# A graph network on one core: thresholds compared inside the steps of the norm, one per engine and step, and edges asked for by fours

## The chip, the core and the metric

The kernel runs on one NeuronCore of a Trainium2 chip. Five engines work beside each other, each in the order of its own queue: PE (TensorE, matrix products), DVE (VectorE), ACT (ScalarE), POOL (GpSimd) and SP (SyncE, which here only issues transfers). Transfers run on 16 DMA engines; they are issued by SP, by ACT, and by POOL for indirect ones (gathers by a list of addresses). Semaphores hold an instruction until what it needs is there.

The metric is the device time of one execution in microseconds (us), the median of several runs. Before the change it is 2130.42 us (three runs, 2127.44 to 2132.5).

## The reference, cut to what matters

```python
def agg(h):
    return jax.ops.segment_sum(h[src], dst, num_segments=N)      # N = 6250, 100000 edges, dst sorted

h = jnp.maximum(_layernorm(x), 0.0)                              # x: 6250 x 256
y = h
for l in range(3):
    h = y + agg(y)
    h = relu(h @ W1s[l] + b1s[l]); h = relu(h @ W2s[l] + b2s[l])
    y = h @ W3s[l] + b3s[l]
h = y + agg(y)
h = relu(h @ cW1 + cb1); h = relu(h @ cW2 + cb2)                 # cW2: 256 x 64
return x + h @ cW3 + cb3
```

## The kernel before, in words

The 6250 nodes are 49 blocks of 128. The sum over edges is done as a product with a matrix of edge counts, block by block: `build` makes the counts of a block (128 destinations against all nodes) as products of one-hot rows, `product_by_node` and `product` multiply them with the node values (XY, a high and a low part), and some blocks are gathered instead, by indirect transfers of rows (`Gathered`). The first matrix of each layer is applied ahead of the sum, and W3 of a layer is multiplied with W1 of the next one (`fused`).

All of that needs a preparation, and the change lies in it. Three generators share it; the order in which they are advanced is written out by hand under `tc.manual_schedule()` (from L964 on), and it is the order of each engine's queue.

- `look` finds the edges. It loads the first destination of each 128 edges (`firsts_i`), spreads them over 98 partitions by a product (L652), counts how many lie below each partition's first node (L654) and so finds where a partition's edges begin. Each partition (64 nodes) loads a window of NEAR edges from there with one indirect transfer (`near_i`, L663). In the window it counts, for 17 thresholds four nodes apart, the edges below the threshold: 11 of them on DVE (L695), 6 on ACT by a sign (L698). From the counts come the starts of 16 groups; for each group the destinations and the sources are asked for with `ask` (L611, 32 indirect transfers on POOL), and 14 more for the blocks that are gathered. Lines L720 to L757 place these. Then come four pieces of 4 groups each (L773 to L779, and transposes L786), a check that the list is sorted (L794, L795, on `run`, the whole list), checks of the counts (L800 to L820), and the gathered blocks' addresses (L826 to L845). A violated check sets `wrong`, and a general path then computes everything anew.
- `fused` turns W3 (L575, L577), multiplies it (L586), with the bias as an additional left side (b3b, L579), and copies and stores the result (L588, L589). It runs in six halves.
- `normed` does the layer norm and the first product with W1 over 25 pairs of blocks. In step s it copies the product of pair s-3 out (`out`, L932, every third on ACT, the rest on DVE), splits pair s-4 in a high part (L936, ACT) and a low one (L940, DVE), scales pair s (L899, ACT), transposes pair s-1 (L908, copied by ACT L911), multiplies pair s-2 (L920), takes the moments of pair s+6 (L879, L880, DVE) and stores pair s-5 (SP). `settle` turns moments into scales (L891, L892).

Before, `look` goes through all of its thresholds first, with the halves of `fused` between ACT's six, and then the steps of the norm start; the remaining parts of `look` are put behind single steps (`STAGES`). Each step first asks for two transfers of edges; each waits for the latest product of the norm (`after`), so that they are spread.

Behind the norm's last store, `build` makes the first one and a half blocks (12 batches, 24 copies out of PSUM, L1084 on ACT and L1086 on DVE in turns), and then the products begin.

Loads carry one of eight semaphores, in rotation; an issue waits until the load that had the same one has landed.

Of the kernel before, what the change touches and what calls it, by code (L numbers as in the profile page):

```python
# [8 lines left out]
F32 = mybir.dt.float32  # L9
# [5 lines left out]
OP = mybir.AluOpType  # L15
# [381 lines left out]
def sorted_edges(  # L397
# [63 lines left out]
    NEAR = 11 * P  # L461
# [95 lines left out]
    def fused(pool, w3_aps, w1_aps):  # L557
# [11 lines left out]
        for l in range(NLAYER):  # L569
            w3, w1 = loaded[l]  # L570
            w3t = pool.tile([P, KC, C], F32, name="w3t", bufs=1)
            for k in range(KC):
                ps = ps_m.tile([P, W], F32, name="ps")
                for i in range(KC):
                    nc.tensor.transpose(ps[:, i * P:(i + 1) * P], w3[:, i, k * P:(k + 1) * P],  # L575
                                        ident)
                nc.scalar.copy(w3t[:, k, :], ps[:, :C])  # L577
            b3b = pool.tile([P, KC, P], F32, name="b3b", bufs=1)
            nc.gpsimd.tensor_copy(b3b, b3[l][:, :, None].to_broadcast([P, KC, P]))  # L579
            yield  # L580
            w = pool.tile([P, KC + 1, C], F32, name="w31", bufs=1)
            for i in range(KC + 1):
                ps = ps_m.tile([P, W], F32, name="ps")
                for k in range(KC):
                    left = w3t[:, k, i * P:(i + 1) * P] if i < KC else b3b[:, k, :]
                    nc.tensor.matmul(ps[:, :C], left, w1[:, k, :], start=(k == 0),  # L586
                                     stop=(k == KC - 1))
                nc.scalar.copy(w[:, i, :], ps[:, :C])  # L588
# [28 lines left out]
    def look(pool):  # L617
        firsts_i = pool.tile([1, EB], I32, name="near_i", bufs=1)
        with nc.allow_non_contiguous_dma(reason="each tile's first destination"):
# [6 lines left out]
        nc.sync.dma_start(out=run[:FULL, :], in_=bass.AP(tensor=dst.tensor, offset=dst.offset,  # L626
                                                         ap=[[EC, FULL], [1, EC + 1]]))
        nc.sync.dma_start(out=run[FULL:FULL + 1, :E - FULL * EC],
                          in_=dst[FULL * EC:E].rearrange("(o e) -> o e", o=1))
# [15 lines left out]


        half = pool.tile([P, 2], F32, name="half", bufs=1)
        junk = pool.tile([P, NEAR], BF16, name="junk", bufs=1)
        for h in range(2):
# [3 lines left out]
                             start=True, stop=True)  # L653
            nc.vector.tensor_scalar(junk[:NSUB, e0:e1], ps[:NSUB, :e1 - e0], low[:NSUB, 0:1], None,  # L654
# [11 lines left out]
        )  # L666
        yield
# [24 lines left out]
        DV = 11  # L692
        for q in range(GSUB + 1):
            if q < DV:
                nc.vector.tensor_scalar(junk[:NSUB], near[:NSUB], float(GD * q), None,  # L695
                                        op0=OP.is_lt, op1=OP.add, accum_out=less[:NSUB, q:q + 1])
            else:
                nc.scalar.activation(junk2[:NSUB], near[:NSUB], AF.Sign, bias=edge[:NSUB, q:q + 1],  # L698
                                     accum_out=less[:NSUB, q:q + 1])
                yield  # L700
        nc.vector.tensor_scalar(less[:NSUB, DV:], less[:NSUB, DV:], -0.5, float(NEAR // 2),
                                op0=OP.mult, op1=OP.add)
        first = pool.tile([P, GSUB + 1], F32, name="first", bufs=1)
        nc.vector.tensor_scalar(first[:NSUB], less[:NSUB], at[:NSUB, 0:1], None, op0=OP.add)
        starts = pool.tile([NSUB, GSUB], I32, name="starts", bufs=1)
        nc.vector.tensor_scalar(starts, first[:NSUB, :GSUB], float(E - P), None, op0=OP.min)
        wd = pool.tile([P, GSUB, P], I32, name="wd", bufs=1)
        ws = pool.tile([P, GSUB, P], I32, name="ws", bufs=1)
        for q in range(GSUB):
            for w, e in ((wd, dst), (ws, src)):  # L710
                asks.append((w[:NSUB, q, :], e, starts[:, q:q + 1]))
        ask(4)
# [4 lines left out]
        sel = pool.tile([P, NQ, PW], F32, name="near_i", bufs=1)  # L717
# [113 lines left out]
        yield  # L831
# [27 lines left out]
    def normed(pool, ps_t, ps_z):  # L859
        G = 6  # L860
# [86 lines left out]
        for t0 in range(0, 4 * G, G):  # L947
            load(t0)
        yield
        for s in range(G):  # L950
            moments(s)
        settle(G)
        yield
        for s in range(len(pairs) + 5):
            if s % (G // 2) == 0 and s and s * 2 + 3 * G < NT:
                load(s * 2 + 3 * G)
            for lag, f in ((3, out), (4, high), (0, scale), (1, turn), (2, times), (-G, moments),
                           (4, low), (5, keep)):
                if 0 <= s - lag < len(pairs) and (f is not moments or s - lag >= G):
                    f(s - lag)  # L960
            settle(s + G - 1)
            yield

    with tc.manual_schedule():  # L964
        with tc.tile_pool(name="prep", bufs=2) as prep, tc.tile_pool(
# [88 lines left out]
        def build(hots, ats, ps_b):  # L1054
# [7 lines left out]
            for k, (s, q0) in enumerate(batches):  # L1062
# [6 lines left out]
                for q in range(0, BATCH, 2):  # L1069
# [13 lines left out]
                    if step % 2:  # L1083
# [705 lines left out]
```

## Time and profile before

| | us |
|---|---|
| median of three runs | 2130.42 |
| the profiled execution | 2135.8 |
| its span | 2134.0 |
| first product (L1588) starts | 142.70 |
| first one-hot (L1035) starts | 126.08 |
| first compare with a threshold (L695) | 23.77 |
| first scaling of the norm (L899) | 43.48 |

A row of the timeline gives start, duration, engine, line, operation, output and input with their shapes, and the number of instructions merged into it; in brackets stands the idle time of the engine ahead of it and what ended that. A row of groups gives the count, the busy time, the mean duration of one in ns and the idle time ahead. Consecutive instructions of one engine overlap in the records by about 0.1 us, so that what one costs is better read from its start to the start of the next. A row of windows gives a stretch, the busy time of each engine in it, the granted clock of PE and the use of the DMA engines.

### The profile page before, as it was taken

The numbers are of one execution on the slowest core, as the hardware profiler recorded it, in microseconds if no ns is written. First come the engines' busy times: TensorE is split into PE (matmuls) and PEld (weight loads), VectorE is DVE, ScalarE is ACT, GpSimd is POOL, SyncE is SP. The second block draws the span as 40 slices with busy tenths as digits, with TensorE's granted clock in tenths as the row PEclk, the third lists the DMA queues.
The fourth block names the chain that finished last, engine by engine and source line by source line (L and its number), as shares of the span: only waits on it lengthen the run. The fifth ranks groups of instructions, "written<-read, shape, count | busy, mean of one in ns | idle before, by whom it ended". The sixth has DMA issues, their size and how long they took to land.

```text
span 2134.0 us, 33393 instructions
## 1 busy us (share of the span) xinstructions
PE 2057.4 (96%) x12076; PEld 1487.8 (70%) x12076; DVE 937.7 (44%) x2192; ACT 864.3 (41%) x1775; POOL 1445.4 (68%) x1470
## 2 busy tenths in 40 slices
PE   4979999999999999999999999999999999999997
PEld 3756766667667777777776777777776777777675
DVE  7877867667673422222233322222233433333332
ACT  4856655556556522323232433222333432223231
POOL 2727777777774477777776377777776277777773
PEclk9979999999999999999999999999999999999999
DMA  5524545545455655455455554555456555556553
GB/s 157 176 98 139 162 142 153 158 140 164 150 158 152 213 163 155 153 181 164 142 186 167 173 160 148 173 165 169 146 168 195 170 172 181 184 180 194 183 160 119
DMA packets 184901, 347.61 MB, mean 163 GB/s; under 512 B 32446, under 2 KB 118496, under 8 KB 184726
## 3 DMA queue, kind: packets, MB, share of 16 engines
q0 software_dynamic: 68960, 185.41, 29.7%
q1 hardware_dynamic: 113838, 158.12, 22.3%
q8 instruction: 97, 1.59, 0.3%
q10 hardware_dynamic: 1928, 1.85, 0.3%
q14 instruction: 78, 0.64, 0.1%
HBM read 287.98 MB, written 57.26 MB: 162 GB/s over the span
## 4 chain that ended last, share of the span: by engine, by line
PE 88%; DVE 5%; DMA 4%; issue 1%; ACT 1%; POOL 1%; SPq 0%; DVEq 0%; POOLq 0%; ACTq 0%
PE agg L1665 43%; PE agg L1588 16%; PE sums L1419 11%; PE ps L1233 6%; PE ps L1290 6%; PE bp L1076 4%; DMA rows<-table,idx 3%; PE ps L1479 1%; POOL rows L1382 1%; DVE junk L695 1%; PE bp L920 1%; DVE hi L1035 1%; DVE at L1086 1%; PE ps L1245 0%; DMA table<-zs 0%
## 5 line engine op out<-in xcount | busy, mean ns | idle before, releaser
L1382 POOL DMA_INDIRECT rows<-table,idx x1394 | 1387.7, 995 | 611.4 <-issue 220.6
L1665 PE MATMUL agg<-a,XY 128*128 128x512 f32 x4116 | 982.8, 395 | 1.9 <-DVE clT L1600 1.9
L1665 PEld LDWEIGHTS agg<-a,XY 128*128 128x128 f32 x4116 | 764.6, 188 | 209.5 <-issue 45.8
L1565 ACT CAST a<-at 128x512 fp32r<-128x512 uint8 (+1 forms) x542 | 326.9, 616 | 576.9 <-PE agg L1665 543.9
L1565 DVE CAST a<-at 128x512 fp32r<-128x512 uint8 x543 | 242.7, 448 | 552.8 <-PE agg L1665 469.3
L1588 PE MATMUL agg<-XY,a 128*128 128x512 f32 x1470 | 404.9, 409 | 1.3 <-DVE un L1600 0.7
L1588 PEld LDWEIGHTS agg<-XY,a 128*128 128x128 f32 x1470 | 258.9, 189 | 53.7 <-issue 8.7
L1419 PE MATMUL sums<-rows,hot 128*32 128x256 f32 x3772 | 256.0, 385 | 16.2 <-DMA rows<-table,idx 15.0
L1419 PEld LDWEIGHTS sums<-rows,hot 128*32 128x32 f32 x3772 | 112.6, 109 | 142.6 <-issue 53.6
L1549 ACT CAST a<-at 128x512 fp32r<-128x512 uint8 (+2 forms) x362 | 196.7, 574 | 6.5 <-PE agg L1588 6.5
L1084 ACT CAST at<-bp 128x392 uint8<-128x392 f32 x240 | 116.6, 487 | 203.7 <-PE bp L1076 191.0
L1086 DVE CAST at<-bp 128x392 uint8<-128x392 f32 x240 | 135.1, 563 | 138.2 <-PE bp L1076 138.2
L1448 DVE TENSOR_TENSOR u<-u,sums 128x256 f32<-128x256 f32 x82 | 34.3, 419 | 241.8 <-PE agg L1665 226.9
L1076 PE MATMUL bp<-hi,lo 128*128 128x196 bf16 x960 | 127.5, 255 | 11.0 <-DVE hi L1035 10.7
L1290 PE MATMUL ps<-w,h 128*128 128x256 f32 x588 | 133.9, 379 | 1.4 <-ACT h L1236 0.9
L1233 PE MATMUL ps<-h,w 128*128 128x512 f32 (+3 forms) x332 | 133.9, 545 | 0.6 <-DVE zz L1298 0.6
L1035 DVE TENSOR_TENSOR hi<-cols,pairs 128x784 bf16<-128x784 bf16 x240 | 134.3, 560 | 0.0
L1076 PEld LDWEIGHTS <-lo 128*128 128x128 bf16 x960 | 70.6, 99 | 81.9 <-DVE hi L1035 27.8
L1290 PEld LDWEIGHTS ps<-w,h 128*128 128x128 f32 x588 | 111.1, 190 | 18.7 <-ACT h L1236 1.8
L1483 ACT ACTIVATE h<-ps,bias 128x256 f32<-128x256 f32 (+1 forms) x116 | 47.2, 464 | 154.9 <-PE ps L1479 154.9
L1298 DVE TENSOR_TENSOR zz<-ps,w 128x512 f32<-128x512 f32 (+1 forms) x75 | 50.1, 678 | 117.0 <-PE ps L1290 117.0
L1035 DVE TENSOR_TENSOR lo<-lanes,pairs 128x512 bf16<-128x512 bf16 x240 | 100.3, 418 | 1.3 <-ACT pairs L1030 1.3
(171 smaller groups left out, 989.7 us busy)
## 6 DMA issues: line engine op xcount, KB each, us to landing
at<-mat SPq DMA_DIRECT2D x151, 448.0 KB
mat<-at SPq DMA_DIRECT2D x30, 784.0 KB
rows<-table,idx POOLq DMA_INDIRECT x1394
table<-zz SPq DMA_DIRECT2D x72, 256.0 KB
back<-table SPq DMA_DIRECT2D x99, 128.0 KB
xs<-in_x_dram SPq DMA_DIRECT2D x8, 768.0 KB
table<-zs SPq DMA_DIRECT2D x24, 256.0 KB
out_dram<-zz SPq DMA_DIRECT2D x24, 256.0 KB
```

Of the source, the lines that this page charges most:

```text
L1035: nc.vector.tensor_tensor(o.rearrange("p q (n t) -> p q n t", t=2), values.rearrange("p (n t) -> p n t", t=2)[:, None, :, :].to_broadcast( ...
L1076: mm = nc.tensor.matmul(bp[:, m * HW:(m + 1) * HW], lo[:, q + m, :], hi[:, q + m, :], start=True, stop=True)
L1084: nc.scalar.copy(o, v)
L1086: nc.vector.tensor_copy(o, v)
L1233: mm = nc.tensor.matmul(ps[:mp, :w], weights[l][0][:, c, i * P:i * P + mp], h1[:, c, :w], start=(c == 0), stop=(c == KC - 1))
L1290: mm = nc.tensor.matmul(o, h2[0][:, c, nodes], w3[:, c, :], start=(c == 0), stop=(c == KC - 1))
L1382: got = nc.gpsimd.indirect_dma_start(out=t, out_offset=None, in_=tables[self.l][:, :], in_offset=bass.IndirectOffsetOnAxis(ap=idx[:, o:o + ...
L1419: nc.tensor.matmul(self.sums[m * Q:(m + 1) * Q, :C], self.hot[:, (c - min(rounds)) // 2, m, :], self.rows[g, c + 4 * m], start=(c == ROUND ...
L1549: nc.scalar.copy(a[:, i * m * P:(i + 1) * m * P].rearrange("p (j d) -> p j d", j=m), counts[b][:, j:j + m, :])
L1565: cast(o, at[:, :, d:d + m * P])
L1588: mm = nc.tensor.matmul(agg, a[:, d:d + P], XY[:, j, :], start=(j == 0), stop=(j == NT - 1))
L1665: mm = nc.tensor.matmul(agg[c][:, :w], XY[:, j, o:o + P], a[:, :w], start=(j == 0 and half == 0), stop=(j == NT - 1 and half == 1))
```

## The change

- The window NEAR is 1280 edges for 1408.
- The thresholds are compared inside steps 0 to 7 of the norm, one on DVE (the even ones) and one on ACT (the odd ones) a step, the seventeenth on ACT too. After each second step the four groups that are then known are settled (`settled`, three small instructions) and put on the list to be asked for; a step asks for three in steps 1 to 8 and for two later.
- `fused`'s six halves stand behind steps 0 to 5; the bias is read by the product in place, with stride 0, and the copy b3b goes. The biases are turned in step 1.
- The moments run 4 pairs ahead instead of 6. The first pair's stand ahead of the count of the first destinations, three more behind it; x is loaded in two halves, `run` between them.
- ACT issues W3 and W1 of two layers ahead of the biases, then takes a square root into the first column of `wrong`, which loads its table; `look` clears `wrong` behind that in the program.
- The remaining parts of `look` follow other steps, the gathered blocks two by two. `sel` uses another tile.
- The 24 copies of the first batches in `build` are all on ACT.

```diff
-    NEAR = 11 * P
+    NEAR = 10 * P
...
-            b3b = pool.tile([P, KC, P], F32, name="b3b", bufs=1)
-            nc.gpsimd.tensor_copy(b3b, b3[l][:, :, None].to_broadcast([P, KC, P]))
...
-                    left = w3t[:, k, i * P:(i + 1) * P] if i < KC else b3b[:, k, :]
+                    left = (w3t[:, k, i * P:(i + 1) * P] if i < KC else
+                            b3[l][:, k:k + 1].to_broadcast([P, P]))
...
+        for q in range(0, GSUB, 2):
+            nc.vector.tensor_scalar(junk[:NSUB], near[:NSUB], float(GD * q), None,
+                                    op0=OP.is_lt, op1=OP.add, accum_out=less[:NSUB, q:q + 1])
+            for k in (q + 1,) if q + 2 < GSUB else (q + 1, q + 2):
+                nc.scalar.activation(junk2[:NSUB], near[:NSUB], AF.Sign, bias=edge[:NSUB, k:k + 1],
+                                     accum_out=less[:NSUB, k:k + 1])
+            if q % 4 == 2:
+                settled(q - 2, q + 2)
+            if q + 2 < GSUB:
+                yield
+        settled(GSUB, GSUB + 1)
+        yield
...
+            if q % 2 or q == NQ - 1:
+                yield
...
-        G = 6
+        G, LEAD = 6, 4
...
-        for t0 in range(0, 4 * G, G):
+        for t0 in (0, G):
             load(t0)
         yield
-        for s in range(G):
+        moments(0)
+        yield
+        for t0 in (2 * G, 3 * G):
+            load(t0)
+        for s in range(1, LEAD):
             moments(s)
-        settle(G)
+        settle(LEAD - 1)
...
             rows = normed(prep, ps_t, ps_z)
             next(rows)
+            ahead_w = fused(prep, [W3s[l] for l in range(NLAYER)],
+                            [W1s[l + 1] for l in range(NLAYER - 1)] + [cW1])
+            next(ahead_w)
             make_identity(nc, ident)
             nc.vector.memset(eps, EPS)
             turn_biases, (b1, b2, b3) = load_biases(prep)
-            ahead_w = fused(prep, [W3s[l] for l in range(NLAYER)],
-                            [W1s[l + 1] for l in range(NLAYER - 1)] + [cW1])
-            next(ahead_w)
+            nc.scalar.activation(wrong[:, :1], eps, AF.Sqrt)
+            next(looked)
+            next(rows)
             next(looked)
...
+            next(rows)
             next(looked)
-            next(rows)
-            turn_biases()
-            for _ in range(2 * NLAYER):
-                next(looked)
-                next(ahead_w)
-            next(looked)
-            STAGES = (*range(4, 20, 2), 20, 22, 24)
+            STAGES = (*range(10), 10, 11, 12, 13, 15, 16, 18, 19, 20, 21, 22, 23, 24, 25, 26)
             for i, _ in enumerate(rows):
-                ask(2)
+                ask(3 if i < 9 else 2)
+                if i == 1:
+                    turn_biases()
+                if i < 2 * NLAYER + 1:
+                    next(ahead_w, None)
                 if i in STAGES:
                     next(looked, None)
...
-                    if step % 2:
+                    if step % 2 or step <= 2 * PRE:
                         nc.scalar.copy(o, v)
```

More of the change, by code (lines that the diff above doesn't have):

```diff
@@ L691, in look @@
         junk2 = near_i.bitcast(BF16)[:, :NEAR]
[L692 to L700, printed above, removed]
@@ L708, in look, with settled @@
         ws = pool.tile([P, GSUB, P], I32, name="ws", bufs=1)
[L709 to L712, printed above, removed]
+        def settled(q0, q1):
+            odd = slice(q0 + 1 - q0 % 2, q1, 2) if q1 <= GSUB else slice(q0, q1)
+            nc.vector.tensor_scalar(less[:NSUB, odd], less[:NSUB, odd], -0.5, float(NEAR // 2),
+                                    op0=OP.mult, op1=OP.add)
+            nc.vector.tensor_scalar(first[:NSUB, q0:q1], less[:NSUB, q0:q1], at[:NSUB, 0:1], None,
+                                    op0=OP.add)
+            if q1 > GSUB:
+                return
+            nc.vector.tensor_scalar(starts[:, q0:q1], first[:NSUB, q0:q1], float(E - P), None,
+                                    op0=OP.min)
+            for q in range(q0, q1):
+                for w, e in ((wd, dst), (ws, src)):
+                    asks.append((w[:NSUB, q, :], e, starts[:, q:q + 1]))
@@ L956, in normed @@
                 load(s * 2 + 3 * G)
-            for lag, f in ((3, out), (4, high), (0, scale), (1, turn), (2, times), (-G, moments),
+            for lag, f in ((3, out), (4, high), (0, scale), (1, turn), (2, times), (-LEAD, moments),
                            (4, low), (5, keep)):
-                if 0 <= s - lag < len(pairs) and (f is not moments or s - lag >= G):
+                if 0 <= s - lag < len(pairs) and (f is not moments or s - lag >= LEAD):
                     f(s - lag)
-            settle(s + G - 1)
+            settle(s + LEAD - 1)
             yield
```

21 lines of the change are left out of this document (11 added, 10 removed).

## The prediction

> **What bounds the kernel now.** I read the chain of waits first, then the busy time by stage, then the timeline of the preparation. The chain by line, and the five stages between landmarks of the timeline (columns: stretch and its length, busy us of PE, weight load, DVE, ACT and POOL, then the granted clock, the DMA share and GB/s):
>
> ```profile
> PE agg L1665 43%; PE agg L1588 16%; PE sums L1419 11%; PE ps L1233 6%; PE ps L1290 6%; PE bp L1076 4%; DMA rows<-table,idx 3%; PE ps L1479 1%; POOL rows L1382 1%; DVE junk L695 1%; PE bp L920 1%; DVE hi L1035 1%; DVE at L1086 1%; PE ps L1245 0%; DMA table<-zs 0%
> ...
> 0.00:22.80 22.80, 4.29 (x10) 1.83 (x10) 9.68 (x45) 1.95 (x4) 6.46 (x27) 1.00 0.80 238
> 22.80:42.50 19.70, 13.27 (x44) 9.71 (x43) 19.25 (x27) 13.42 (x26) 0.86 (x3) 0.91 0.18 67
> 42.50:48.38 5.88, 3.75 (x28) 2.94 (x27) 4.35 (x23) 3.89 (x9) 4.26 (x5) 0.86 0.29 93
> 48.38:126.08 77.70, 69.81 (x341) 54.97 (x340) 64.14 (x185) 55.74 (x125) 46.17 (x43) 0.92 0.50 150
> 126.08:142.70 16.62, 9.47 (x50) 5.14 (x50) 16.52 (x39) 6.80 (x17) 7.93 (x8) 0.58 0.45 152
> 142.70:2134.00 1991.30, 1956.83 (x11608) 1413.23 (x11608) 823.77 (x1879) 782.53 (x1598) 1379.73 (x1386) 1.00 0.53 164
> ```
>
> After 142.70 us, the first product, PE works 1956.8 of 1991.3 us, and the change touches nothing there. So only the date of the first product counts, and what it gains or loses goes one for one into the span. Before it, DVE is the full engine: 19.25 of 19.70 us while the thresholds are compared (L695), 16.52 of 16.62 while the first one-hots are built. The search for the edges (to 22.8), the compares (to 42.5) and the norm (to 126) stand one behind the other, and the norm alone fills neither PE nor ACT. That is the room for the change.
>
> **Part 1, the start.** The rows of the start, and of the last request for edges with the ACT copy that waits for its landing:
>
> ```profile
> 3.00:5.00 2.00, 0.00 (x0) 0.00 (x0) 0.00 (x0) 0.00 (x0) 0.46 (x1) 1.00 0.21 11
> 10.00:15.00 5.00, 0.24 (x1) 0.00 (x0) 1.25 (x6) 0.00 (x0) 2.96 (x11) 1.00 1.09 348
> ...
> 6.70 0.56 DVE L644 CAST near<-near_i 1x782 f32<-1x782 int32 x1 [5.64 <-DMA near_i<-in_dst_dram]
> 11.65 0.35 SPq L626 DMA_DIRECT2D run<-in_dst_dram  x1
> 12.01 1.19 POOL L663 DMA_INDIRECT near_i<-in_dst_dram,at_i  x1 [8.55 <-DMA brows<-in_L_gnn_b3s_dram]
> 13.91 0.23 ACTq L541 DMA_DIRECT2D brows<-in_L_gnn_cb_dram  x1
> 16.16 1.28 ACT L885 ACT_TABLE_LOAD   x1 [16.16 <-POOL node L683]
> 105.71 1.22 POOL L611 DMA_INDIRECT near_i<-in_src_dram,from_i x1 [0.30 <-issue]
> 108.74 0.30 ACT L830 CAST near<-near_i 17x128 f32<-17x128 int32 x1 [0.84 <-DMA near_i<-in_src_dram,from_i]
> ```
>
> Here the change adds a wait. ACT now does a square root into the first column of `wrong` as its first work, and only behind it in the program DVE clears `wrong`; so DVE's memset waits for ACT, and the cast of the first destinations (6.70 before) and the whole search stand behind that memset. ACT in turn first issues eleven loads. The program hands eight semaphores round among loads, so an issue waits for the landing of the load eight before it: that is why the bias loads trickle out until 13.91, why `run` is issued at 11.65, when the second block of x is down, and why the table load starts at 16.16. In the new order ACT's last two bias loads wait for the two `run` loads. `run` follows the second block in SP's queue: 11.65 + 0.39 MB / 348 GB/s = 12.8. I take it that the four weights now asked for ahead go through while the DMA engines idle (share 0.21 at 3 to 5 us) and delay nothing; if they do delay x, 1.05 MB / 348 GB/s = 3.0 us is the upper end. Two issues of 0.23, the table load of 1.28 and a small activation: the memset at 15.0 (to 18.0). From the cast to the request for `near_i` it took 12.01 - 6.70 = 5.3, so that request goes out at 20.4, 8.4 later than before. Its landing: 3.03 us (108.74 - 105.71) for small rows, plus 98 rows of 5120 B, 0.50 MB at 348 GB/s, 1.4: 24.8. Moments 0 to 4 (10 blocks) and the small integer work, moved here, fill DVE meanwhile, to 25.1. So near can be compared from 25.9, where the old kernel began at 23.8. The norm, though, starts its first `scale` at 23.7 (the offsets at 20.0, six blocks of moments at 0.54 and a settle of 0.4, priced below) instead of 43.5.
>
> **Part 2, steps 0 to 7.** Rows of DVE and ACT; a row's start to the next one's start is its price:
>
> ```profile
> 23.77 1.62 DVE L695 TENSOR_SCALAR_CACHE_REDUCE junk<-near 98x1408 bf16<-98x1408 f32 x1
> 25.44 1.62 DVE L695 TENSOR_SCALAR_CACHE_REDUCE junk<-near 98x1408 bf16<-98x1408 f32 x1
> ...
> 23.83 1.47 ACT L698 ACTIVATE near_i<-near,edge 98x1408 bf16<-98x1408 f32 x1 [1.43 <-POOL b3b L579]
> 25.30 0.62 ACT L577 COPY w3t<-ps 128x256 f32<-128x256 f32 x2
> ...
> 53.82 0.62 ACT L936 CAST XY<-zs 128x512 fp32r<-128x512 f32 x1
> 54.34 1.09 ACT L899 ACTIVATE h<-xs,shift,rstd 128x256 f32<-128x256 f32 x2
> 55.33 0.56 ACT L911 COPY ht<-agg 128x512 f32<-128x512 f32 x1
> ...
> L588 ACT COPY w<-ps 128x256 f32<-128x256 f32 x9 | 3.4, 373 | 5.3 <-PE ps L586 5.2
> ```
>
> DVE's compare falls from 1.67 to 1.52 (1280 columns for 1408), ACT's from 1.47 to 1.36. DVE does 8 instead of 11, ACT 9 instead of 6. ACT is then the longer queue: 8 pairs of h at 0.99, 7 ht at 0.47, 6 zs and XY at 0.52, 9 compares at 1.36, 6 w3t at 0.25, 9 w at 0.27, three roots, the biases and two load issues at about 1.6 together, in all 7.9 + 3.3 + 3.1 + 12.2 + 1.5 + 2.4 + 1.6 = 32.0. To it come waits for PE's groups behind the nine w: between 0 and the 5.2 us of the row; I take 5, near the row, because step 1 has three groups in a PE that has been idle. From 23.7 ACT ends step 7 at 60.7; DVE, 4 x `settled` of three small instructions included, has about 31 us of work there and waits for ACT's last threshold: 60.9. POOL's b3b copies go (0.4 us each, hidden either way); the bias read with stride 0 is a weight load as before, 0 to 0.2 us for each of 12, hidden on PE: taken as 0.
>
> **Part 3, steps 8 to 20.** DVE's rows:
>
> ```profile
> 73.23 0.69 DVE L932 COPY zs<-bp 128x512 f32<-128x512 f32 x1
> 73.83 0.42 DVE L879 BATCH_NORM_STATS2 stats<-xs 128x6 f32<-128x256 f32 x1
> ...
> 74.91 0.66 DVE L940 TENSOR_TENSOR XY<-zs,XY 128x512 fp32r<-128x512 f32 x1
> 75.48 0.68 DVE L932 COPY zs<-bp 128x512 f32<-128x512 f32 x1
> ...
> 77.74 0.18 DVE L891 RECIPROCAL rstd<-std 128x6 f32<-128x6 f32 x1
> ...
> 80.54 0.42 DVE L879 BATCH_NORM_STATS2 stats<-xs 128x6 f32<-128x256 f32 x1
> ...
> 101.06 1.08 DVE L794 TENSOR_TENSOR junk<-run 128x892 bf16<-128x892 int32 x1
> ...
> 105.89 0.17 DVE L800 TENSOR_TENSOR size<-less 98x16 f32<-98x16 f32 x1
> ...
> 107.65 0.27 DVE L826 TENSOR_SCALAR wd<-near_i,base 68x128 f32<-68x128 int32 x1
> ```
>
> Nine zs at 0.60, 25 blocks of moments at 0.54, 13 XY at 0.57, four pieces of edges with their settles at 2.80 (77.74 to 80.54) and one settle more, the placing of the gathered rows 5.88 (the stretch 42.50 to 48.38, its wait for PE included), `down` 2.1 (two of 1.08), the checks 1.76: 5.4 + 13.5 + 7.4 + 11.6 + 5.9 + 2.1 + 1.8 = 47.7. Step 20 ends at 108.6. POOL's 46 requests at 1.27 now start at 35 rather than 43 and go three a step, so that they keep ahead of DVE; no gain taken.
>
> **Part 4, the tail.** Six more products paced by ACT and PE, 2.2 to 2.9 a step, with the fd pieces (0.58 each) two a step between them, then 14 transposes, rel, idx, the last store and its landing: 16 us by the same durations. So the one-hots begin at 124.6 instead of 126.08. The norm gains 1.5 us, of 20 us of overlap: the 8.4 later request takes most, ACT's length in steps 0 to 7 the rest.
>
> **Part 5, the first builds.**
>
> ```profile
> 129.47 0.41 DVE L1035 TENSOR_TENSOR lo<-lanes,pairs 128x512 bf16<-128x512 bf16 x1
> 129.80 0.56 DVE L1035 TENSOR_TENSOR hi<-cols,pairs 128x784 bf16<-128x784 bf16 x1
> 130.28 0.56 DVE L1086 CAST at<-bp 128x392 uint8<-128x392 f32 x1
> 130.76 0.41 DVE L1035 TENSOR_TENSOR lo<-lanes,pairs 128x512 bf16<-128x512 bf16 x1
> ...
> L1084 ACT CAST at<-bp 128x392 uint8<-128x392 f32 x12 | 5.8, 485 | 9.8 <-PE bp L1076 9.8
> ```
>
> Twelve batches at 1.29 on DVE, ACT idle 9.8 us. All 24 copies now go to ACT: DVE needs 0.81 a batch, ACT two copies at about 0.4 (0.485 less the 0.1 by which its rows overlap), PE four matmuls. All three would fit in 0.85 to 1.0: 12 x 0.29 to 0.44, 3.4 to 5.3. I take 4.0, nearer the low end because three engines in step wait for each other.
>
> **The sum.** 1.5 + 4.0 = 5.5 us off. The profiled execution took 2135.8 us, 5.4 over the median of 2130.42, so I take the difference from the median: 2125.
>
> **Rivals.**
> *Weights in the way.* The ahead-loaded weights delay x and `run` by up to 3.0 us, and all behind them: 2.5 us are left, 2128, within 0.2% (4.3 us). For it: nothing in the trace shows them beside the small loads. Against it: the idle DMA at 3 to 5 us. The Trainium skill ("DMA: Bandwidth & Descriptors", Queues, rings and completion order) has each DMA engine take turns between queues, which would put the weights between the first destinations and x; no run here shows it.
>
> *A cold PE, slower.* In the mixed steps PE has gaps. Before, one of 2 us ahead of such a group was followed by this:
>
> ```profile
> 33.44 3.51 PE L586 MATMUL ps<-w1n,w3t 128*128 128x256 f32 x8 [2.01 <-ACT w3t L577]
> ...
> 34.00:37.00 3.00, 3.00 (x10) 2.40 (x9) 2.97 (x4) 1.50 (x4) 0.00 (x0) 0.58 0.27 95
> ```
>
> The granted clock was 0.58 for three to four us. PE's work in steps 1 to 7 is about 27 us at full clock, 54 at half. All cold, step 7 would end near 25 + 54 = 79, 18 us later, so 12 slower: 2142. It decides once over 0.6 of that work runs at half clock. Against it: PE is then busy without a gap. The Trainium skill ("TensorE: Matmul & The Clock Gate", What's actually happening) has the gate open again after some 3.4 us of sustained work, which these rows agree with; by that rule this rival loses.
>
> *The start is not late.* If `wrong` is cleared some 6 us earlier than I read, all of the search moves with it: about 11.5 us off, 2119. For it: little; the semaphore stands in the program.
>
> That the shorter window misses edges and sends the kernel to its general path is no rival: of the 98 windows none but the last, which ends the list and is excused, holds more than 1210 of 1280.
>
> **The numbers.** My forecast 0.50, weights 0.27, cold PE 0.13, early start 0.10. Faster by over 0.2% (about what a measurement here can tell): the first and the last, 0.60; same 0.27; slower 0.13. The range 2115 to 2134 holds the first two and most of the last.
>
> **What would show it.** The cast of the first destinations at 15 to 16 instead of 6.70 and `near_i` requested at about 20; ACT without idling in steps 1 to 7, and nine compares at 1.36; the first one-hot near 124.6, the first product near 137 and ACT full in between. I am wrong if the cast comes early, if the clock is at half over most of 27 to 60 us, or if a DVE wait for requested edges shows from step 9 on.

## The result and the profile after

The changed kernel takes 2136.33 us (median, 2134.7 to 2145.31) beside 2130.74 us (2127.44 to 2135.63) of the old one: a ratio of 1.0026, 95% interval 1.0014 to 1.0039. It is slower, by 5.6 us, where 5.4 us less than the median then known were forecast. The profiled execution took 2138.41 us, its span 2136.6.

The chain of waits by line, and the windows between the landmarks (columns as in the prediction; the stretches are: the start up to the arrival of the window of edges, steps 0 to 7 with compares from there on, step 8, the other steps and the tail, the first builds, the rest):

```profile
PE agg L1685 43%; PE agg L1608 16%; PE sums L1439 11%; PE ps L1310 6%; PE ps L1253 6%; PE bp L1096 4%; DMA rows<-table,idx 2%; POOL rows L1402 1%; PE ps L1499 1%; PE ps L1265 1%; DVE hi L1055 0%; PE ps L1245 0%; PE bp L934 0%; DVE at L1106 0%; DVE lo L1055 0%
...
0.00:29.35 29.35, 5.62 (x13) 2.30 (x14) 8.31 (x39) 3.40 (x7) 6.12 (x26) 1.00 0.61 183
29.35:66.69 37.34, 30.31 (x130) 22.78 (x130) 26.44 (x70) 30.72 (x63) 18.30 (x19) 1.00 0.47 141
66.69:75.74 9.05, 3.82 (x22) 3.55 (x23) 6.75 (x31) 3.82 (x8) 2.57 (x3) 0.58 0.55 162
75.74:130.41 54.67, 49.60 (x256) 38.62 (x254) 50.44 (x144) 40.30 (x92) 29.38 (x26) 0.98 0.40 124
130.41:143.95 13.54, 9.38 (x50) 5.13 (x50) 12.26 (x29) 11.15 (x29) 9.21 (x8) 0.59 0.59 187
143.95:2136.60 1992.65, 1958.82 (x11608) 1414.12 (x11608) 822.46 (x1876) 783.09 (x1598) 1379.89 (x1386) 0.99 0.53 164
```

The first product starts at 143.95, 1.25 us later than in the old kernel's profile (142.70) and 6.75 later than forecast (137.2); behind it the rest is 1.35 longer (1991.3 before). The compares (DVE junk, 1% before) have gone from the chain. In the timeline the late start stands:

```profile
17.28 1.28 ACT L996 ACT_TABLE_LOAD   x1 [17.28 <-DMA brows<-in_L_gnn_cb_dram]
18.84 0.55 DVE L639 CAST near<-near_i 1x782 f32<-1x782 int32 x1 [17.79 <-issue]
24.13 1.19 POOL L660 DMA_INDIRECT near_i<-in_dst_dram,at_i  x1 [20.67 <-DVE stats L893]
27.29 1.09 ACT L913 ACTIVATE h<-xs,shift,rstd 128x256 f32<-128x256 f32 x2 [1.03 <-DVE shift L906]
29.35 0.89 DVE L690 TENSOR_SCALAR near<-near_i,low 98x1280 f32<-98x1280 int32 x1 [0.51 <-DMA near_i<-in_dst_dram,at_i]
```

| | before | forecast | after |
|---|---|---|---|
| cast of the first destinations | 6.70 | 15 to 16 (to 18.0) | 18.84 |
| request for `near_i` | 12.01 | 20.4 | 24.13 |
| first scale | 43.48 | 23.7 | 27.29 |
| steps 0 to 7 | | 37.2 long, to 60.9 | 39.4 long, to 66.69 |
| steps 8 to 20 | | 47.7 long, to 108.6 | 48.2 long, to 114.92 |
| first one-hot | 126.08 | 124.6 | 130.41 |
| first product | 142.70 | 137.2 | 143.95 |

### The profile page after: what moved, and what is told of

It is laid out like the page before. It is cut to its first block, busy times and chain, and to the rows that moved or that the text cites. A ratio compares the mean times of both kernels' runs of the same rounds, so it can differ in the third digit from the quotient of the medians.

```text
span 2136.6 us, 33393 instructions
## 1 busy us (share of the span) xinstructions
PE 2057.6 (96%) x12076; PEld 1486.5 (70%) x12076; DVE 926.7 (43%) x2185; ACT 872.5 (41%) x1794; POOL 1445.5 (68%) x1467
## 4 chain that ended last, share of the span: by engine, by line
PE 87%; DVE 2%; DMA 2%; issue 1%; POOL 1%; ACT 1%; DVEq 0%; SPq 0%; POOLq 0%; ACTq 0%
PE agg L1685 43%; PE agg L1608 16%; PE sums L1439 11%; PE ps L1310 6%; PE ps L1253 6%; PE bp L1096 4%; DMA rows<-table,idx 2%; POOL rows L1402 1%; PE ps L1499 1%; PE ps L1265 1%; DVE hi L1055 0%; PE ps L1245 0%; PE bp L934 0%; DVE at L1106 0%; DVE lo L1055 0%
## 5 line engine op out<-in xcount | busy, mean ns | idle before, releaser
L1439 PEld LDWEIGHTS sums<-rows,hot 128*32 128x32 f32 x3772 | 111.6, 109 | 141.2 <-issue 53.1
L1104 ACT CAST at<-bp 128x392 uint8<-128x392 f32 x252 | 121.1, 488 | 197.3 <-PE bp L1096 184.0
L1106 DVE CAST at<-bp 128x392 uint8<-128x392 f32 x228 | 128.4, 563 | 140.4 <-PE bp L1096 140.4
```

Source lines behind the costliest of these rows:

```text
L1104: nc.scalar.copy(o, v)
L1106: nc.vector.tensor_copy(o, v)
L1439: nc.tensor.matmul(self.sums[m * Q:(m + 1) * Q, :C], self.hot[:, (c - min(rounds)) // 2, m, :], self.rows[g, c + 4 * m], start=(c == ROUND ...
```

## The experiments

My theory: the start is late twice over, since the search waits for ACT's root and since the weights, asked for ahead, hold up the loads for which ACT waits. The rivals: the mixed steps themselves are too long, or PE is too cold, whenever they start. The runs were made in four groups, each on one chip with the old kernel beside it, and each ratio is to that old kernel; kernels that are compared here are not always of one group. The first group (the weights behind, the root apart, and the first two runs of the copies) ran on a chip on which the old kernel takes 2363.1 us (PE waits there for its own issue, which is 5% of the chain); of those I use the preparation's trace and the ratio. On the other three chips the old kernel takes 2130.6 to 2131.7.

**The weights behind the biases.**

```diff
-            next(ahead_w)
             make_identity(nc, ident)
...
             nc.scalar.activation(wrong[:, :1], eps, AF.Sqrt)
+            next(ahead_w)
             next(looked)
```

> The changed kernel, but ACT issues the four weights of `fused` behind the biases and the square root in place of ahead of them. Theory (the weights stand in the way of x and of `run`, and so of the bias loads ahead of the root): the first block of x lands near 9.3 as in the old kernel (12.97 in the changed one), the cast of the first destinations comes at 14 to 16 (18.84), which is what the prediction took; the first product 3 to 4 us earlier, time 2132 to 2133.5. Rival (the weights are not what is late): the cast stays at 18 or later and the time within 1 us of the changed kernel. If the weights are then late themselves, step 0 to 2 of `fused` will show it as waits of PE for w3.

SP's issues of x and of `run` in the changed kernel, and ACT's first bias:

```profile
1.62 7.34 SPq L516 DMA_DIRECT2D xs<-in_x_dram  x2
9.08 0.46 SPq L664 DMA_DIRECT2D run<-in_dst_dram  x1
12.97 0.51 ACTq L538 DMA_DIRECT2D brows<-in_L_gnn_b1s_dram  x1
```

The same with the weights behind:

```profile
1.62 3.76 SPq L516 DMA_DIRECT2D xs<-in_x_dram  x2
...
5.42 0.54 SPq L664 DMA_DIRECT2D run<-in_dst_dram  x1
...
13.85 1.28 ACT L993 ACT_TABLE_LOAD   x1 [13.85 <-DMA brows<-in_L_gnn_cb_dram]
15.40 0.55 DVE L639 CAST near<-near_i 1x782 f32<-1x782 int32 x1 [14.36 <-issue]
20.70 1.18 POOL L660 DMA_INDIRECT near_i<-in_dst_dram,at_i  x1 [17.25 <-DVE stats L893]
23.86 1.09 ACT L913 ACTIVATE h<-xs,shift,rstd 128x256 f32<-128x256 f32 x2 [1.03 <-DVE shift L906]
```

The four weights nearly double the time that SP spends on issuing two blocks of x (7.34 for 3.76), `run` follows 3.7 us later, and with it the last biases, the table load and the cast. It is the issue that is held, and not only the data. A window of the changed kernel, then the same two us with the weights behind:

```profile
7.00:9.00 2.00, 0.00 (x0) 0.00 (x0) 0.00 (x0) 0.00 (x0) 0.00 (x0) 1.00 0.17 21
```

```profile
7.00:9.00 2.00, 0.00 (x0) 0.00 (x0) 0.00 (x0) 0.00 (x0) 0.00 (x0) 1.00 1.08 380
```

With the weights ahead, SP is still issuing x until 8.96 while the DMA engines move next to nothing (21 GB/s); without them x and `run` are already on their way (380 GB/s). What holds SP's issue is not shown. Without them in the way the start is the forecast to some tenths: cast 15.40, request 20.70, first scale 23.86. First product at 140.55, 3.4 earlier. Ratio 0.9986 (0.9972 to 1.0000); the changed kernel was not timed on that chip. The theory holds for this half.

**The root in a tile of its own.**

```diff
-            nc.scalar.activation(wrong[:, :1], eps, AF.Sqrt)
+            nc.scalar.activation(warm, eps, AF.Sqrt)
```

> The changed kernel, but the square root that loads ACT's table writes a tile of its own, so that clearing `wrong`, and the search behind it on DVE, no longer waits for ACT. Theory (the late start costs the time): the cast of the first destinations (18.84 in the changed kernel) comes when its load is down, at 6 to 10; `near_i` is requested at 12 to 15 (24.13); the first scale still waits for ACT's table, so it comes at 20 to 22 (27.29), and everything behind it, the first product too, 5 to 7 us earlier; time 2129 to 2131. Rival (the interleaved steps or the transfers bound the start anyway): the cast comes early but the first product moves by under 2 us; time 2134.5 or more.

```profile
9.48 0.56 DVE L640 CAST near<-near_i 1x782 f32<-1x782 int32 x1 [8.42 <-DMA near_i<-in_dst_dram]
15.88 1.18 POOL L661 DMA_INDIRECT near_i<-in_dst_dram,at_i  x1 [12.43 <-DVE stats L894]
19.13 1.09 ACT L914 ACTIVATE h<-xs,shift,rstd 128x256 f32<-128x256 f32 x2 [0.46 <-DVE shift L907]
```

The cast waits only for its own load, the request goes out 8.2 us earlier, the first scale at 19.13, the first product at 136.14, 7.8 earlier than in the changed kernel. Ratio 0.9952 (0.9933 to 0.9971) on that chip. From the first scale to the first one-hot it takes 103.2 us, for 103.1 in the changed kernel, so what the start loses the first product loses.

**Both together, and a price that nobody asked for.** The edit is the two above.

> The changed kernel with the root in a tile of its own and the weights behind the biases and the root. Theory (two separate delays at the start, the wait for ACT and the weights in the way, that add): cast of the first destinations at 6.5 to 7.5, `near_i` requested at 12 to 13.5, first scale at 16 to 18 (ACT's table loaded near 14), first product at 133 to 134.5, 10 us before the changed kernel. Rival (from the root's freedom on, the moments on DVE or the landing of x bound the start): the first scale stays at 19 as with the root alone moved, and the first product at 136.

First scale 17.78 and first product 133.70, as the theory had it, 9.6 us earlier than in the repeat of the changed kernel (143.26). And yet 2137.27 us, a ratio of 1.0024 (1.0013 to 1.0034): no gain at all. The part behind the first product took 2005.2 us. The groups of the products (count, busy us, mean ns) told where: the same 4116 products took 400 ns for 395. Apart from the order of the start, the edit had only added a tile of four bytes (`warm`) in the middle of the constants. So I added only that:

```diff
     one = const.tile([P, 1], F32, name="one")
+    const.tile([P, 1], F32, name="warm")
```

> The changed kernel with a tile of four bytes added among the constants that nothing uses; no instruction differs but for addresses. Theory (addresses): first product at 143.3 to 144 as in the changed kernel, the part behind it 8 to 14 us longer, time 2144 to 2150. Rival (addresses without effect): 2136 to 2138.

And, with the weights behind as before, gave the root a place in the padding that the constants have anyway:

```diff
-    const.tile([P, 96], U8, name="align")
+    pad = const.tile([P, 96], U8, name="align")
...
-            nc.scalar.activation(wrong[:, :1], eps, AF.Sqrt)
+            nc.scalar.activation(pad.bitcast(F32)[:, :1], eps, AF.Sqrt)
```

> The kernel with both delays of the start gone once more, but the root writes into the padding that the constants already have, so that no tile behind it moves. Theory (the four bytes of the new tile moved the operands of the products and cost 12 us there): first product again at 133 to 134.5, the part behind it back at 1988 to 1992, `agg` from `a` and XY at a mean of 395 ns and not 400, time 2125 to 2128. Rival (products that start earlier lose it again, on gathers or on their own order): the part behind stays at 2000 or more, time 2135 or more.

The groups behind the first product, the repeat of the changed kernel first (it ran on another chip than the two below it):

```profile
L1685 PE MATMUL agg<-a,XY 128*128 128x512 f32 x4116 | 981.6, 395 | 1.8 <-DVE clT L1620 1.8
L1585 DVE CAST a<-at 128x512 fp32r<-128x512 uint8 x543 | 241.3, 446 | 551.9 <-PE agg L1685 471.7 <-PE agg L1608 37.8 <-ACT a L1585 31.1
```

With the four bytes:

```profile
L1686 PE MATMUL agg<-a,XY 128*128 128x512 f32 x4116 | 1001.7, 399 | 1.9 <-DVE clT L1621 1.9
L1586 DVE CAST a<-at 128x512 fp32r<-128x512 uint8 x543 | 247.7, 458 | 561.0 <-PE agg L1686 484.3 <-PE agg L1609 38.4 <-ACT a L1586 26.8
```

With the root in the padding:

```profile
L1685 PE MATMUL agg<-a,XY 128*128 128x512 f32 x4116 | 983.0, 395 | 1.8 <-DVE clT L1620 1.8
```

Four unused bytes cost 12 us: 2148.52 us, ratio 1.0089 (1.0076 to 1.0102), with the first product at 143.44 as ever and 2000.1 us behind it. The root apart, above, had the same four bytes: on its chip these products took 405 ns for 401 with the weights behind, but the part behind was only 1.4 us longer (2216.3 for 2214.9), so what the bytes cost there stays open. With the root in the padding the part behind is 1992.1 again and the time 2129.74, ratio 0.9994 (0.9983 to 1.0005). That is 7 us better than the changed kernel (2136.8, 1.0028) and what the late start cost, but no more than equal to the old kernel. It was 2 us more than I expected; its first product came at 136.26, not 133.7. In that execution `near_i` landed 1.2 later, and PE was cold for longer around step 8 (granted clock 0.58 over 59 to 71, for 0.66 over 59 to 69 in the kernel with `warm`). The preparation of one and the same order thus varies by 2.6 us between these two profiles.

**The two kernels once more.** No edit.

> The changed kernel itself, for a further trace and for its time beside the others here. Theory: the preparation repeats to some tenths (first scale 27.3, first one-hot 130.4, first product 143.9), and what separates it from the old kernel by more than the first product's 1.25 us lies behind the first product. Rival: the preparation itself varies by several us from run to run.

> The old kernel itself, for a further trace. Theory: the first product again at 142.7, and the 5.4 us by which its first profiled execution lay above the median of its runs are in the part behind the first product (1991.3 then, some 1986 here on a chip of the same speed). Rival: the norm of the old order varies (its first one-hot came at 134.85 in the old kernel with other copies, 126.08 in the old kernel's first trace), and the first one-hot comes at 134 to 135 here too.

The changed kernel repeats: 130.15, 143.26, 1990.8 behind; 2136.8 us, ratio 1.0028 (1.0017 to 1.0039). The old one does not. Its first one-hot came at 122.57 and its first product at 139.19, 3.5 earlier than in the profile on which I forecast. Two rows of DVE and one window in the old kernel's first profile:

```profile
92.64 0.69 DVE L932 COPY zs<-bp 128x512 f32<-128x512 f32 x1 [1.43 <-DMA table<-zs]
122.18 0.69 DVE L932 COPY zs<-bp 128x512 f32<-128x512 f32 x1 [2.69 <-PE bp L920]
...
110.00:120.00 10.00, 8.36 (x32) 6.53 (x33) 6.34 (x19) 4.60 (x10) 0.00 (x0) 0.58 0.23 79
```

and in the repeat, which has no such wait for a store:

```profile
118.68 0.69 DVE L932 COPY zs<-bp 128x512 f32<-128x512 f32 x1 [0.60 <-PE bp L920]
...
110.00:120.00 10.00, 8.62 (x42) 7.12 (x43) 6.89 (x19) 4.48 (x9) 0.00 (x0) 0.83 0.23 79
```

The half-clock stretch of the first profile, then the stretch of the repeat in which the clock was back:

```profile
111.70:121.80 10.10, 9.28 (x32) 7.52 (x33) 4.75 (x13) 3.58 (x7) 0.00 (x0) 0.50 0.23 78
```

```profile
115.00:122.50 7.50, 6.79 (x40) 5.45 (x38) 4.74 (x13) 3.23 (x8) 0.00 (x0) 1.00 0.26 86
```

The norm of the old order has two lengths. By 110 us the repeat is 0.7 us ahead; in front of that, the visible difference is the wait of 1.4 us for the buffer that a late store still holds. PE's waits around 110 to 112 are alike in both (1.36 and 1.37 us, 1.34 and 1.38), and the clock falls to half near 111.6 in both. In the repeat it is back after some 3.4 us, in the first profile only after some 10, and that makes the other 2.8 us. Why it came back early in the one and not in the other is not shown. On chips of this speed four profiles of the old order show first one-hots at 126.08, 122.57, and below 126.09 and 121.98: two of each. My second theory for this run (the surplus of 5.4 us lies behind the first product) falls for half of it: of the 6.8 us between the spans of the two profiles (2134.0 and 2127.2) 3.5 lie in front of the first product and 3.3 behind it.

**The copies alone**, in the old kernel, and in turns again in the changed one:

```diff
-                    if step % 2:
+                    if step % 2 or step <= 2 * PRE:
```

> The old kernel with only the 24 copies of the first builds all on ACT. Theory: the builds shrink from 16.62 us by 3.1 as in the changed kernel, and the clock of PE, which has stayed at half through them, costs the products behind 1.35 us of it: 1.5 to 2.5 us less than the old kernel. Rival (the colder PE is a matter of the changed kernel's norm, not of the builds): the full 3.1 us or more less. Rival (the first builds are not on the path): no change.

> The changed kernel with the copies of the first builds on ACT and DVE in turns again. Theory: the builds take 16.6 us again in place of 13.54, the products behind get 1.35 us back: 1.5 to 2.5 us more than the changed kernel, 2138 to 2139. Rival (the copies are without effect): within 0.5 us of the changed kernel.

> The old kernel with only the 24 copies of the first builds on ACT, beside the others here. Theory: the builds take 13.55 for 16.62, and the products behind give 1 us back: 2128.5 to 2130, 1.5 to 3 us less than the old kernel. First one-hot of the old order at 122.5 to 126, so first product at 136 to 139.5.

The builds took 13.55, 16.63 and 13.49: the copies are worth 3.1 us there, on either kernel. The ratios, 0.9975 (0.9964 to 0.9987), 0.9997 (0.9983 to 1.0011) and 0.9986 (0.9977 to 0.9995), the last being 2127.48 us, put the part at 3 us of gain in the old kernel on the last chip and at 6 on the slower one; what putting the turns back costs the changed kernel stays open, since that was not timed on the slower chip. Of the 3.1 some is given back. In the timeline the row that holds the 120th product starts 42.6 us behind the first product with the old builds, 44.0 us with the short ones in the last of these runs and in the changed kernel's first profile; other profiles with short builds on chips of this speed have 42.6 to 43.3.

**PE kept busy in the first builds.** One product that nobody reads behind each group, in the changed kernel and in the old one with the copies on ACT:

```diff
                     passed(BUILD, mm)
+                    if step < 2 * PRE:
+                        still = ps_m.tile([P, W], F32, name="ps")
+                        nc.tensor.matmul(still, XY[:, 1, :P], XY[:, 0, :], start=True, stop=True)
```

> The changed kernel with one more product of 512 columns, whose result nobody reads, behind each of the 24 groups of the first builds, so that PE has no gaps there. Theory (the gaps of PE in the shorter builds leave it at half clock into the first products, 1.4 us): granted clock 1.00 within 4 to 6 us of the builds' start, 120 products behind the first one in 42.6 us or less for 44.0, builds of 13 to 14 us, time 1 to 2 us under the changed kernel, 2134.5 to 2135.5. Rival (the added products hold up the builds): the builds take 15 us or more, and no gain.

> The old kernel with the 24 copies on ACT and PE kept busy in the first builds. Theory: 1 to 1.5 us less than with the copies alone (2127.5), 2126 to 2126.5, for 120 products in 42.6 us in place of 44.0. If the interleaving of the norm and the thresholds has a worth of its own, the kernel with all of it is faster than this one by 2 us or more; if not, the two are within 1 us.

The ten us from the first product on: the old kernel with short builds, the changed kernel with PE busy, the old one with short builds and PE busy:

```profile
139.58:149.58 10.00, 10.00 (x40) 7.17 (x40) 4.84 (x13) 6.03 (x13) 0.18 (x1) 0.69 0.00 0
```

```profile
142.94:152.94 10.00, 10.00 (x57) 7.49 (x58) 7.15 (x19) 7.96 (x18) 2.04 (x3) 1.00 0.18 61
```

```profile
135.42:145.42 10.00, 10.00 (x57) 7.46 (x58) 7.13 (x18) 7.92 (x18) 2.01 (x3) 1.00 0.18 60
```

40 products became 57, the clock 1.00 for 0.69, and the row of the 120th product starts 41.1 to 41.2 us behind the first: 2.8 less than with short builds, 1.4 less than with the old ones, which had been cold too. In these two profiles the clock is 1.00 through all of the builds, and they are no longer for it (13.45, 13.44). The changed kernel goes to 2134.27 (1.0012, 1.0000 to 1.0023), the old one to 2123.24 (0.9966, 0.9955 to 0.9977), 4.3 us by the ratios where I expected 1 to 1.5. Half clock at the first products is thus what the short builds gave back, and it cost the old builds too, which I had not seen. The first 120 products are not all of it: behind the first product the old kernel's profile takes 1984.3 us for 1990.9, 6.6 less, of which they hold 2.8. Part of the rest lies at later dips of the clock (0.97 over 1135 to 1185 with PE busy, 0.93 over 1140 to 1190 without); whether that follows from the added products is not shown.

**ACT's length in steps 0 to 7.** Thresholds 1, 5 and 9 on DVE for ACT, in the kernel with both delays gone and `warm` in place:

```diff
-            nc.vector.tensor_scalar(junk[:NSUB], near[:NSUB], float(GD * q), None,
...
+            extra = (q + 1,) if q in (0, 4, 8) else ()
+            for k in (q, *extra):
+                nc.vector.tensor_scalar(junk[:NSUB], near[:NSUB], float(GD * k), None,
...
```

> As the kernel with both delays gone, but the thresholds are divided as in the old kernel, 11 on DVE and 6 on ACT (thresholds 1, 5 and 9 go from ACT to DVE). Theory (ACT's queue is the length of steps 0 to 7): these steps become 2 to 4 us shorter, since ACT loses 3 of 1.36 us and DVE has room, and the first product comes 2 to 4 us earlier, at 130 to 132. Rival (the waits for PE's groups, or DVE, bound the steps): under 1 us earlier, or later.

First product 133.51 for 133.70, 2135.85 us for 2137.27. The rival holds: ACT lost 4.1 us of work (three of 1.36), but from the first scale to DVE's first instruction of the placing it took 41.6 us (17.26 to 58.87) for 41.3 (17.78 to 59.10). So ACT's work alone is not the length of these steps; which wait took its place was not followed up.

**PE's stall at step 8.** In the changed kernel PE's small products for the gathered rows (L750) stand in its queue behind step 8, and DVE's comparisons for them stand behind DVE's step 8:

```profile
71.92 1.75 PE L750 MATMUL ps<-both,f 98*68 98x6 f32 x14 [6.56 <-DVE f L747]
```

```diff
         nc.vector.tensor_tensor(sel[:NSUB], sel[:NSUB], some[:NSUB], OP.mult)
+        yield
         ps = ps_m.tile([P, W], F32, name="ps")
...
-            STAGES = (*range(10), 10, 11, 12, 13, 15, 16, 18, 19, 20, 21, 22, 23, 24, 25, 26)
+            STAGES = (*range(10), 10, 11, 12, 13, 14, 15, 16, 18, 19, 20, 21, 22, 23, 24, 25, 26)
```

> As the kernel with the root in the padding and the weights behind, and the placing of the gathered rows is cut in two: its seven small products and what follows stand one step of the norm behind the comparisons that they wait for on DVE. Theory (in the changed kernel PE stands behind these products for 6.6 us, falls to half clock for the 9 us behind it, and the norm waits for PE): no stall of PE there, granted clock 1.00 through 50 to 75 us, first product 3 to 5 us earlier, at 129 to 131, and the time as much lower, 2121 to 2124. Rival (DVE is the length of the norm from there on, whatever PE does): first product at 132.5 or later.

The nine us behind step 7 without the cut, and with it:

```profile
57.60:66.60 9.00, 2.44 (x19) 2.34 (x19) 5.97 (x24) 4.66 (x9) 3.69 (x4) 0.68 0.59 169
```

```profile
57.00:66.00 9.00, 6.85 (x36) 5.28 (x37) 7.89 (x28) 7.31 (x15) 5.31 (x6) 0.81 0.61 172
```

The 6.6 us are gone, the first product comes at 133.87 (2.4 earlier), and the time is 2126.95, ratio 0.9976 (0.9967 to 0.9985), 2.8 us under the median of the kernel without the cut; the two intervals overlap a little. That is less than the 3 to 5 us and the 2121 to 2124 of the theory, and by its number (132.5 or later) the rival holds: the stall was worth far less than its 6.6 us. The 2.4 us at the first product are no proof by themselves, since the kernel with `warm` came to 133.70 with the stall in place.

**The halves of `fused` one step later**, since PE now waited 9.8 us for the late W3; then that and the busy builds together:

```diff
-                if i < 2 * NLAYER + 1:
+                if 1 <= i < 2 * NLAYER + 2:
```

> As the kernel with both delays gone and the placing cut in two, with the halves of `fused` behind steps 1 to 6 for 0 to 5. Theory (the weights, now asked for late, hold PE for 9.8 us, and ACT's copy behind it): no wait of PE for W3, step 1 some 2 to 4 us earlier, first product at 130 to 132, time 2123.5 to 2125.5. Rival (the bound of steps 0 to 7 is ACT's work, and of 8 to 20 DVE's): first product within 1 us of 133.9 and the time of 2127 kept.

> Both together: `fused` one step later and PE kept busy in the first builds. Theory: the two add, 1 to 2 us less than with `fused` later alone, 2122 to 2124.5. Rival: no gain from the added products where the clock comes back early by itself; the same time as with `fused` later alone.

The wait of PE for W3 fell to 0.2 us and nothing came of it, as the rival had it: first product 133.53, 2126.70 us, ratio 0.9977 (0.9965 to 0.9989). With PE busy in the builds: 2120.97 us (six runs), ratio 0.9948 (0.9928 to 0.9967), 5.7 us less where I expected 1 to 2. It beats the old kernel by 9.7 us on this chip, and the changed one by some 15 across chips. Its profile does not say why by so much: the builds took 14.99 us there, and the first product came at 136.21, later than the 133.53 without the added products. The old order with the same builds, on the same chip, is 2.3 us behind (2123.24), with intervals that overlap, and in its profile the first product comes at 135.42, before this one. Other profiles of the new order without the two delays have 133.5 to 136.3, those of the old order with short builds 135.4 and 139.6. So the interleaving may be worth some us of its own, but these runs do not separate it from the spread.

## Why the prediction was wrong

- **Part 1, the start: the term that failed first.** The wait for ACT's root and its path were right. The sentence "I take it that the four weights now asked for ahead go through while the DMA engines idle and delay nothing" was wrong, and its upper end of 3.0 us too small: with the weights taken away the cast, the request and the first product came 3.4 us earlier, and the first scale of the changed kernel lay 3.6 behind the forecast. The rival *weights in the way*, to which I had given 0.27, named the cause; its 2128 is 8 us short of the time measured. The Trainium skill ("DMA: Bandwidth & Descriptors", Queues, rings and completion order) has each DMA engine take turns between queues, which I had put beside that rival. These rows do not show turns: over 7 to 9 us SP was still issuing x and the engines moved 21 GB/s.
- **The baseline.** "The profiled execution took 2135.8 us, 5.4 over the median, so I take the difference from the median" assumed that the surplus lies behind the first product. The repeat reached its first product 3.5 us earlier: my profile held the old norm's longer variant. Measured against the shorter one, my forecast of the changed preparation (137.2) gained 2.0 us, not 5.5.
- **Part 2, steps 0 to 7: 2.2 us short.** ACT's work came to 32.3 us for 32.0 and its waits for PE's groups to 5.0 for 5:

```profile
ACT w L587 <- PE ps L585: 5.0, 5, 1.9
ACT near_i L717 <- DVE near L690: 1.4, 1, 1.4
...
ACT near_i L717 <- ACT w L587: 0.6, 1, 0.6
```

  What I left out is the second row: ACT's first sign stands in its queue ahead of step 1 and waits 1.4 us for the edges, which come later than the first scale. In the third row ACT stands still while it issues two loads. That the steps are ACT's length alone was wrong as well: with three compares fewer on ACT they were as long.
- **Part 3, steps 8 to 20: 48.2 for 47.7.** The sum came out, but by its parts it hides a stall: PE idle for 6.6 us and at 0.58 of its clock over step 8, in place of the 5.88 of DVE that I had put there. Cutting the step in two gave 2.8 us by the medians.
- **Part 4, the tail: 15.5 for 16.** Right.
- **Part 5, the builds: 3.1 for 4.0,** and up to 1.4 given back by the half clock behind them. That the products behind are untouched by the change was wrong by this.
- **The gain of the interleaving.** "That is the room for the change" looked at PE and ACT. From the first compare to the first one-hot the old order takes 98.8 (23.76 to 122.57), the new one 100.1 (30.06 to 130.15). DVE alone is busy for 86.5 of those 98.8, so of the 20 us of overlap no more than DVE's gaps of 12.3 were ever to be had. The profiles fit that: with both delays of the start gone, the first one-hot came at 119.8 to 122.8, against 122.0 and 122.6 in the shorter variant of the old norm.
- *A cold PE* as stated, in steps 1 to 7, is false: clock 1.00 from 29.35 to 66.69. Cold stretches there are, but at step 8 and in the builds. *The start is not late* is false.

Added up against the changed kernel's first profile: 3.6 (start) + 2.2 (steps 0 to 7) + 0.5 - 0.5 + 0.9 (builds) = 6.7 of the 6.75 at the first product. The 11.0 us between a forecast of 5.4 less and a result of 5.6 more are made up of these, of up to 3.5 of the baseline and of up to 1.4 of the half clock.

## What to carry to other kernels

A wait that is added at the head of a program is priced by every load ahead of it in its issuing queue, and loads asked for early are not free because the DMA engines idle at that moment: here they held up the issue of a transfer that was urgent. Before a gain of a few us is forecast, see how much the old kernel's own profile varies in the very stretch that is changed, and which engine is full there; overlapping two stretches that both fill the same engine gives only its gaps. Where PE waits between short groups just ahead of the main loop, some products without a reader can be worth more than the shorter wait: here 4.3 us by the ratios, against 3 for the shorter builds.

## What the hardware showed that I had not expected

- Four unused bytes among the constants, by which the tiles allocated behind them presumably move: 11.7 us (2136.8 to 2148.5 against nearly equal old kernels), the products 399 ns for 395, the cast of the counts 458 for 446. Which operand it is, and why, was not tried.
- Kept busy, PE was at half clock for some 3.4 us here. In the fastest kernel the first pair of products in the builds, at 122.17, still takes 0.33 us; then the pairs take 0.55, with PE kept busy, and at 125.96 it is 0.35 again. The last row is the window in between:

```profile
122.17 0.33 PE L1097 MATMUL bp<-hi,lo 128*128 128x196 bf16 x2 [2.31 <-DVE hi L1056]
...
122.69 0.55 PE L1097 MATMUL bp<-hi,lo 128*128 128x196 bf16 x2
...
125.17 0.55 PE L1097 MATMUL bp<-hi,lo 128*128 128x196 bf16 x2
...
125.96 0.35 PE L1097 MATMUL bp<-hi,lo 128*128 128x196 bf16 x2
```

```profile
122.48:125.89 3.41, 3.41 (x14) 2.03 (x12) 2.28 (x5) 2.08 (x5) 2.49 (x4) 0.50 0.72 255
```

  That is 3.4 us at half clock of unbroken work; the Trainium skill ("TensorE: Matmul & The Clock Gate", What's actually happening) has about 3.4 us of sustained work, and agrees. Short groups with gaps, 9.4 us of work in 13.5, left the clock at 0.59 over the builds of the changed kernel's first profile. In its repeat the clock was back for a while in the middle of the builds (1.00 over 137.0 to 140.3) and was lost again, so that the same short groups can go either way.
- One chip ran the old kernel in 2363 us for 2131, with a granted clock of 0.97 for 0.99, and with PE waiting for its own issue. The cause was not looked for.
